# A 3x3 convolution moved into the next image's attention stretch, and the scan's sums, gather and output projection queued one step later

## The chip, the core and the metric

The kernel runs on one core of a Trainium2 chip. Its engines have a queue of instructions each, worked off in order: PE (matrix products, into PSUM), DVE (vector work), ACT (activations, with a table that must be loaded for some functions), POOL (vector work and indirect DMAs), SP (here only DMA issues). The metric is device microseconds for one execution, the median of several runs.

## What is computed

An image has 256 channels of 32 x 32 points, and there are four. Layer one is, for every image:

```python
xn = layernorm(xs)                                   # over channels
xm = mamba_v(xc, ...) + skip_scale * xc              # 4 groups of 64 channels, scan over 1024 points
Q  = conv1d(conv1d(x_concat, qdw), qpw); xg = sigmoid(Q) * xm
R  = conv1d(conv1d(xgt, rdw), rpw) + xgt
xm2 = conv1d(conv1d(cat, fdw), fpw) + cat[:, :Cc]
x_local  = conv1d(xm2, lc)
x_global = mha(xm2)                                  # 8 heads of 32
x_out = gelu(layernorm(concat(x_local, x_global) @ fc_w.T))
xi = conv3x3_depthwise(ln_hw(x_out))
x  = x + layernorm(xi) @ proj_w.T
```

Layer two is a mixture of eight experts with two chosen for each of the 4096 points: a gate picks them, and each expert is 256 to 1024, gelu, 1024 to 256. The scan is h = dA * h + dBu over the points, 128 inner channels times 16 states for each group.

## The kernel before

**Scan.** An image is 8 parts: 4 groups (n), 2 halves (h) of 512 points. A part is 16 steps (`scan`, L631): a step multiplies dt*u by B on DVE (L538), runs the scan instruction on DVE (L545) and multiplies by C on POOL (L550, and L549 keeps the last column in the first half). dA comes from ACT (L531). Every fourth step, `sums_of` (L552) adds up states on PE (L556). Around this, tables written by hand say at which step of a part other pieces are queued: `before` (L583) holds the finish of the part before (last sums, `gather` L561 with a POOL multiply, `project_out` L568, `add_skip` L573), `behind` and `group` what the next part needs.

**Everything else** is written as Python generators: each `yield n` ends a piece, and the next piece is issued n beats later. `beat()` (L1166) moves all running generators on; a scan step is followed by one beat. So the order on each engine's queue is fixed when the program is built. Buffers come from pools with tags: "a8" (8 buffers of 128 x 2048), "a4" (7), "a2" (17 of 128 x 512: dA, hs, the exponentials e of attention, squares), and 8 PSUM banks.

**Order of an image b.** In the first four parts of image b the scan runs beside `convolutions(b-1)` (L684): the depthwise passes of L360 and the rdw, rpw, fdw, fpw products. At the end of part 3 the scan stops, and `attention(b-1)` (L842) runs in 32 steps: logits on PE (L861), exponentials on ACT (L871), values on PE (L903), pair sums on DVE (L913), column sums on PE (L881). Beside it run `local(b-1)` (L927), the end of part 3, and `normalised(b+1)` (L382). When step 29 is queued the flag "attended" is set and the scan goes on with parts 4 to 7. `mixing(b-1)` (L936) follows attention in the same generator: output projection and fc (L947 to L967), a layer norm and gelu (L990 to L998), statistics (L1001 to L1014), the 3x3 taps (16 DVE instructions, L1035), a second layer norm, the projection and the residual (L1049 to L1071), and the dispatch of the image's rows to experts (L1414): transposes, gate, places, and 16 indirect DMAs on POOL (L1539).

**Tail.** `tiles` (L1081) starts in the last part of image 3. It loads expert weights, reads 256 rows (L1688), transposes them (L1734) and runs a tile: 32 products (L1757), gelu on ACT (L1762), 32 products (L1767), and two indirect adds on POOL (L1778). 35 tiles run this way, in series of 8, 8 and 23 less 4: the first series needs images 0 and 1 counted and sent, the second image 2, the third image 3. `known` and `sent` (L1088, L1091) test that, and a tile that isn't loaded polls every fourth beat. After the scan, `convolutions(3)` runs beside the tiles; then the flag "hold" stops the tiles, `attention(3)` runs, and `mixing(3)` runs beside the tiles again, with the speed of the tiles against it set by `PACE`. Tile 15 is held until image 3 is sent.

Of the kernel before, what the change touches and what calls it, by code (L numbers as in the profile page):

```python
# [10 lines left out]
AF = mybir.ActivationFunctionType  # L11
ALU = mybir.AluOpType
# [4 lines left out]
NC2 = C // P  # L17
# [54 lines left out]
def network(  # L72
# [27 lines left out]
    nc = tc.nc  # L100
    shifted = sums is None
    B = x.shape[0]
# [25 lines left out]
    eps5 = cpool.tile([P, 1], F32, name="eps5")  # L128
# [14 lines left out]
    with tc.tile_pool(name="w_conv", bufs=1) as wp, tc.tile_pool(  # L143
        name="act8", bufs=8
    ) as act8, tc.tile_pool(name="act4", bufs=7) as act4, tc.tile_pool(
        name="act2", bufs=17
    ) as act2, tc.tile_pool(name="steps", bufs=2) as actd, tc.tile_pool(
        name="steps4", bufs=6
    ) as acts, tc.tile_pool(name="rows", bufs=3) as actc, tc.tile_pool(
        name="small", bufs=1  # L150
    ) as small, tc.tile_pool(
        name="spread", bufs=2, space=bass.MemoryType.DRAM
# [23 lines left out]
        for i in range(4):  # L176
            at = _AT["qk_b"] + i // 2
# [58 lines left out]
        GD, GS = DIN // 32, DS // 4  # L236
# [62 lines left out]
        def a8(name):  # L299
            return act8.tile([P, NC2, N], F32, tag="a8", name=name)  # L300
# [127 lines left out]
        T = {}  # L428
# [144 lines left out]
        def add_skip(b, n, h):  # L573
# [7 lines left out]


        before = {  # L583
            1: [(sums_of, GS - 1)], 3: [(gather,)], 6: [(project_out,)], 8: [(add_skip,)],
        }

        behind = {
# [43 lines left out]
        def scan(at, i, stop):  # L631

            b, n, h = parts[at]
            q, g = divmod(i, GD)
            if at > 0:
                for what, *args in before.get(i, ()):
                    if parts[at - 1] not in finished:
                        what(*parts[at - 1], *args)
            if at + 1 < len(parts):
                for what, *args in behind.get(i, ()):  # L640
                    if what is not spread_b or not stop:
                        what(*parts[at + 1], *args)
            nb, nn = (b, n + 1) if n + 1 < NB else (b + 1, 0)
            if nb < B:
                for what, *args in group[h].get(i, ()):
                    what(nb, nn, *args)
            if g == 1 and q + 1 < GS:
                spread_b(b, n, h, q + 1)
            if g == 0 and q + 1 < GS:
                spread_c(b, n, h, q + 1)  # L650
            if g == 1 and q > 0:
                sums_of(b, n, h, q - 1)
            ahead = i + LEAD
            if ahead < NSTEP:
# [272 lines left out]
        def local(b):  # L927

            yield 3
            XLOC[b] = a8(f"xloc_{b}")  # L930
            for c in range(NC2):
                yield from depthwise3(XLOC[b], c, XM2[b], c, "lc_w", c, col("lc_b", c))
            del XM2[b]


        def mixing(b):  # L936

            xloc, oT = XLOC.pop(b), OT.pop(b)
            xglo = a8(f"xglo_{b}")

            def pace(ticks):

                if b == B - 1:
                    T["pace",] = ticks

            pace(PACE["product"])
            yield from in_turn(  # L947
                CO_H, lambda at: product(
                    f"ao_{b}_{at[0]}_{at[1]}", aoutT_s, at[0],
# [4 lines left out]
                ),  # L954
            )

            xc = a8(f"xc_{b}")
            both = (xloc, xglo)
            yield from in_turn(
                CO_H, lambda at: product(  # L960
# [5 lines left out]
                ),  # L966
            )  # L967

            def inverse_deviation(name):
                r = a4(f"r_{name}")  # L970

                def squares(h):
                    sq = [a2(f"sq_{name}_{h}_{c}") for c in range(NC2)]
                    for c in range(NC2):
                        nc.scalar.activation(sq[c], xc[:, c, half(h)], AF.Square)
                    return sq

                for h in range(2):
                    sq = squares(h)
                    yield 1  # L980
                    var = column_mean(f"var_{name}_{h}", sq)
                    yield 2
                    root(r[:, half(h)], var, eps5)
                    yield 1
                yield 1
                for c in range(NC2):
                    nc.vector.tensor_tensor(xc[:, c, :], xc[:, c, :], r, ALU.mult)
                    yield 1

            pace(PACE["norm"])  # L990
            yield from inverse_deviation(f"lgn_{b}")
            for c in range(NC2):
                nc.scalar.activation(
                    xc[:, c, :], xc[:, c, :], AF.Gelu, bias=col("lgn_b", c), scale=col("lgn_w", c)
# [2 lines left out]
            log_exp()  # L997
            yield 2  # L998


            mv = small.tile([P, NC2, 2], F32, tag="mv", name=f"mv_{b}")  # L1001
            for c in range(NC2):
                st = small.tile([P, 2, 6], F32, tag="bn", name=f"bn_{b}_{c}", bufs=2)
# [8 lines left out]
                rs[:, :, 1:2], mv[:, :, 0:1], -1.0, rs[:, :, 0:1], ALU.mult, ALU.mult  # L1012
            )
            yield 1  # L1014
            xi = a8(f"xi_{b}")
            xz = []
            pace(PACE["taps"])
            for c in range(NC2):
                xz.append(
                    act4.tile([P, HH, WW], F32, tag="a4", name=f"xz_{b}_{c}")  # L1020
# [17 lines left out]
                    )  # L1038
                    yield 1 if k % 2 else 0

            xc = xi

            def centre(h, mean):
                for c in range(NC2):
# [1 line left out]
                        xc[:, c, half(h)], xc[:, c, half(h)], mean, ALU.subtract  # L1046
                    )

            pace(PACE["norm"])  # L1049
            xr = a8(f"xr_{b}")  # L1050
            nc.sync.dma_start(xr, x[b].rearrange("(c p) n -> p c n", p=P))
            yield from in_turn(
# [4 lines left out]
            yield from inverse_deviation(f"fin_{b}")  # L1057

            def residual(at, r):
                co, h = at  # L1060
# [11 lines left out]
            pace(PACE["rows"])  # L1072
# [5 lines left out]
            pace(1)  # L1078


        def tiles():  # L1081
# [81 lines left out]
        def start(*what):  # L1163
            running.extend([tick, w] for w in what)
# [17 lines left out]
        def one_by_one(*what):  # L1182
            for w in what:
                yield from w

        def flagged(what, *flag):
            yield from what
            T[flag] = True
# [10 lines left out]
        PACE = {"product": 3, "norm": 1.7, "taps": 0.67, "rows": 1.6}  # L1199
        with tc.manual_schedule(engines=ALL):  # L1200
            log_exp()
            start(normalised(0), weights())
            drain()
            first_part()
            for b in range(B):
                for p in range(PARTS):
                    at = b * PARTS + p
                    stop = b > 0 and p == PARTS // 2 - 1 or at == len(parts) - 1
                    if b == 0 and p == 2:
                        start(normalised(1))  # L1210
                    if b > 0 and p == 0:
                        start(convolutions(b - 1))
                    if at == len(parts) - 1:
                        start(tiles())
                    for i in range(NSTEP):
                        scan(at, i, stop)
                        if b > 0 and p == 0 and i == 9:
                            whole(b - 1)
                        beat()
                    if b > 0 and p == PARTS // 2 - 1:  # L1220
                        drain()
                        behind_ = [attention(b - 1), mixing(b - 1)]
                        start(one_by_one(*behind_), finish_part(at), local(b - 1))
                        if b + 1 < B:
                            start(normalised(b + 1))
                        while not T.get(("attended", b - 1)):
                            beat()
                        resume(at + 1)
            T["scanned",] = True
            start(  # L1230
                flagged(finish_part(len(parts) - 1), "whole", B - 1),
                flagged(convolutions(B - 1), "convolved"),
            )
            until("convolved")
            T["hold",] = True
            until("held")
            start(flagged(attention(B - 1), "attended", B - 1, 2), local(B - 1))
            until("attended", B - 1, 2)
            T["hold",] = False
            start(mixing(B - 1))  # L1240
            drain()

    if not shifted:
# [23 lines left out]
class Experts:  # L1267
# [10 lines left out]
    T = 256  # L1278
# [627 lines left out]
```

## Time and profile before

| | us |
|---|---|
| median of 3 runs (2509.42 to 2511.86) | 2511.09 |
| the profiled execution | 2513.66 |
| its span, first to last instruction | 2511.8 |
| PE, DVE, ACT, POOL busy | 2124.0, 1632.1, 1192.2, 1160.5 |
| scan from its first step to its last | 81.2 to 1723.3 |
| parts with an attention in them (images 1, 2, 3) | 129.8, 129.8, 117.9 |
| tail | 1723.3 to 2511.8 |

How to read the lines that follow. A line of the stretch view has the stretch (us from the span's start), its length, and then for each engine the busy us and the instructions; behind that the granted PE clock, the share of the DMA engines and GB/s. A line of the group view has the line of the kernel, engine, operation, output and inputs by name, shapes and count; behind the bar the busy us and the mean ns of one; behind the second bar the idle time just ahead of them. PE's busy time is modelled for pipelined products, so that a full PE need not be at its peak.

### The profile page before, as it was taken

To read this page: it belongs to the slowest core of one execution; us is meant where nothing else is said; L and a number is where in the kernel's file an instruction comes from. 1 tells how busy PE (TensorE), PEld (TensorE's weight loads), DVE (VectorE), ACT (ScalarE), POOL (GpSimd) and SP (SyncE) were. 2 spreads that over 40 slices of the span, in tenths; PEclk is the share of its full clock that TensorE was granted. 3 is DMA by queue.
4 is the path that set the end of the run, shared out by engine and by line. 5 is a ranking of instruction groups with operands and counts; after the bars stand their busy time and mean duration, and the time that the engine had idled before them with its cause. 6 is when DMAs were issued, how large, how long until landed. Compare 5 with 4: busy or idle time off the path is not lost. (4 is left out here: it accounts for less than half of the span.)

```text
span 2511.8 us, 28315 instructions
## 1 busy us (share of the span) xinstructions
PE 2124.0 (85%) x8810; PEld 945.7 (38%) x8810; DVE 1632.1 (65%) x2243; ACT 1192.2 (47%) x2014; POOL 1160.5 (46%) x1163
## 2 busy tenths in 40 slices
PE   5776778899977879997786999758899999699995
PEld 2111111333312213331221322214674366588884
DVE  2688898875799997578999766897324434311111
ACT  1544455368645534776444478632325853222221
POOL 2577777541576595146758613663421011322221
PEclk8788897899978879998787999979999999899997
DMA  3443342320233233022342210333443034666664
GB/s 94 98 112 96 85 117 70 73 68 26 51 89 98 72 102 89 9 59 65 85 110 85 66 42 22 81 108 123 142 112 89 1 93 143 192 194 193 193 197 147
DMA packets 154540, 244.17 MB, mean 97 GB/s; under 512 B 34016, under 2 KB 103300, under 8 KB 154376
## 3 DMA queue, kind: packets, MB, share of 16 engines
q1 hardware_dynamic: 133856, 215.46, 30.4%
q0 software_dynamic: 13744, 19.31, 3.8%
q10 hardware_dynamic: 6776, 7.45, 0.9%
q8 instruction: 74, 1.21, 0.2%
q14 instruction: 90, 0.74, 0.1%
HBM read 141.16 MB, written 33.85 MB: 70 GB/s over the span
## 5 line engine op out<-in xcount | busy, mean ns | idle before, releaser
L550 POOL TENSOR_TENSOR hs<-hs,cs 128x512 f32<-128x512 f32 x512 | 687.6, 1344 | 215.7 <-DVE hs L545 160.0
L531 ACT ACTIVATE dA<-dts,A 128x512 f32<-128x512 f32 x512 | 344.5, 715 | 285.2 <-DMA dts<-dt 191.0
L556 PE MATMUL yp<-hs,quads 128*32 128x512 f32 x1024 | 317.4, 677 | 162.2 <-POOL hs L550 124.0
L538 DVE TENSOR_TENSOR dBu<-dts,bs 128x512 f32<-128x512 f32 x512 | 348.6, 681 | 67.3 <-DMA dts<-dt 24.2
L1778 POOL DMA_INDIRECT Y<-ys,dest x70 | 113.5, 1622 | 582.2 <-DVE ys L1777 430.6
L545 DVE TENSOR_TENSOR_SCAN hs<-dA,last,dBu 128x512 f32<-128x512 f32 x256 | 327.7, 1280 | 24.6 <-DVE dBu L538 0.5
L545 DVE TENSOR_TENSOR_SCAN hs<-dA,dBu 128x512 f32<-128x512 f32 x256 | 312.5, 1221 | 33.5 <-ACT dA L531 8.6
L1762 ACT ACTIVATE hs<-h,b 128x256 f32<-128x256 f32 x280 | 117.2, 472 | 425.9 <-PE h L1757 222.0
L871 ACT ACTIVATE e<-st 128x512 f32<-128x512 f32 x512 | 263.4, 605 | 94.9 <-PE st L861 94.5
L1767 PE MATMUL y<-w,hs 128*128 128x256 f32 x1120 | 263.8, 388 | 8.9 <-ACT hs L1762 8.9
L1757 PE MATMUL h<-xT,w 128*128 128x256 f32 x1120 | 252.6, 381 | 0.0
L549 POOL COPY last<-hs 128x1 f32<-128x1 f32 x256 | 92.5, 361 | 311.8 <-DVE hs L545 305.1
L1767 PEld LDWEIGHTS y<-w,hs 128*128 128x128 f32 x1120 | 215.0, 195 | 46.8 <-ACT hs L1762 11.0
L913 DVE TENSOR_TENSOR e<-e,e 128x512 f32<-128x512 f32 x256 | 177.0, 753 | 79.1 <-PE av L903 61.6
L1757 PEld LDWEIGHTS h<-xT,w 128*128 128x128 f32 x1120 | 212.5, 191 | 40.6 <-issue 9.7
L1735 DVE COPY xT<-xp 128x512 f32<-128x512 f32 x35 | 24.2, 691 | 303.5 <-PE xp L1734 292.9
L523 PE MATMUL bs<-u,xpwT_s 128*32 128x512 f32 x1024 | 181.0, 677 | 35.1 <-DVE hs L545 29.9
L556 PEld LDWEIGHTS yp<-hs,quads 128*32 128x32 f32 x1024 | 52.9, 119 | 389.2 <-POOL hs L550 263.6
L861 PE MATMUL st<-qk 32*128 32x512 f32 x1024 | 188.5, 647 | 4.7 <-DVE hs L545 4.5
L439 PE MATMUL up<-xn,inwk 64*128 64x512 f32 x256 | 149.0, 733 | 18.4 <-DVE hs L545 12.3
L903 PE MATMUL av<-e,v 128*32 128x512 f32 x1024 | 141.1, 615 | 0.0
L861 PEld LDWEIGHTS st<-qk 32*128 32x128 f32 x1024 | 67.0, 185 | 125.5 <-issue 81.0
(271 smaller groups left out, 2522.9 us busy)
## 6 DMA issues: line engine op xcount, KB each, us to landing
w<-in_W_dram SPq DMA_DIRECT2D x136, 512.0 KB
dts<-dt SPq DMA_DIRECT2D x512, 128.0 KB
cs<-cd SPq DMA_DIRECT2D x512, 64.0 KB
xs<-XS SPq DMA_DIRECT2D x35, 260.0 KB
b<-in_b_dram SPq DMA_DIRECT2D x35, 128.0 KB
xn<-in_x_dram SPq DMA_DIRECT2D x4, 1024.0 KB
XL<-xl SPq DMA_DIRECT2D x8, 512.0 KB
xl<-XL SPq DMA_DIRECT2D x4, 1024.0 KB
```

The costliest lines, as they stand in the source:

```text
L439: nc.tensor.matmul(up, inwk[rows, c, k, :], XN[b][rows, c, ds(k + h * HALF, HALF)], start=(k == 0), stop=(k == KC - 1),)
L523: nc.tensor.matmul(bs[r], xpwT_s[:, n, s : s + 1].to_broadcast([P, 32]), T[b, n, "u"][:, half(h)], start=True, stop=True,)
L531: nc.scalar.activation(dA, T[b, n, h, "dts", g][:, 0, :], AF.Exp, scale=A[:, g, n, q : q + 1])
L538: nc.vector.tensor_tensor(dBu, T[b, n, h, "dts", g][:, 1, :], T[b, n, h, "bs", q], ALU.mult)
L545: nc.vector.tensor_tensor_scan(hs, T[b, n, h, "dA", i], dBu, 0.0 if h == 0 else last, ALU.mult, ALU.add)
L550: nc.gpsimd.tensor_tensor(hs, hs, T[b, n, h, "cs", q], ALU.mult)
L556: nc.tensor.matmul(T[b, n, h, "yp"][ts(g, 32)], quads, T[b, n, h, "hs", q * GD + g], start=(q == 0), stop=(q == GS - 1),)
L861: nc.tensor.matmul(sts[i], k[r, ts(kt, P)], q[r, half(h)], start=True, stop=not shifted)
L871: nc.scalar.activation(es[i], sts[i], AF.Exp, scale=1.0 / HD**0.5)
L913: nc.vector.tensor_tensor(first[i], first[i], es[i], ALU.add)
L1757: nc.tensor.matmul(hp[:, i, :], w1(c, k), xT[:, c, :], start=(c == 0), stop=(c == NC2 - 1))
L1767: nc.tensor.matmul(yp[:, ts(t, C)], hs[:, k, ts(t, P)], w2(k), start=(k == 0), stop=(k == NHC - 1))
```

## The change

`mixing` is cut in three. `joined(b)` holds the output projection, fc, layer norm and gelu; `around(b)` the statistics and the 3x3 taps; `sent_off(b)` the second layer norm, projection, residual and dispatch. `attention(b-1)` is now followed by `joined(b-1)` alone. `around(b-2)` runs behind `local(b-1)`, beside `attention(b-1)`, and for b = 2 `normalised(b+1)` is queued behind it in that generator. `sent_off(b-2)` waits for a flag: "joining" (the fc products of b-1 are queued) for image 2, "attending" (`joined` has begun) for image 3. Image 2's `around` and `sent_off` run after the scan, beside `convolutions(3)` and the first tiles; image 3's follow `joined(3)` as before. `xc` is handed on through the dictionary XC, and its buffer is held that long.

In the scan, `sums_of`, `gather`, `project_out` and `add_skip` are queued one step later, and the flag for `convolutions` with them. What each piece issues is the same.

```diff
         before = {
-            1: [(sums_of, GS - 1)], 3: [(gather,)], 6: [(project_out,)], 8: [(add_skip,)],
+            2: [(sums_of, GS - 1)], 4: [(gather,)], 7: [(project_out,)], 9: [(add_skip,)],
         }
...
-            if g == 1 and q > 0:
+            if g == 2 and q > 0:
                 sums_of(b, n, h, q - 1)
...
-        def mixing(b):
+        def joined(b):
 
             xloc, oT = XLOC.pop(b), OT.pop(b)
+            pace(b, PACE["product"])
             xglo = a8(f"xglo_{b}")
-            pace(PACE["product"])
+            T["attending", b] = True
...
-            xc = a8(f"xc_{b}")
+            xc = XC[b] = a8(f"xc_{b}")
...
+            T["joining", b] = True
+            pace(b, PACE["norm"])
+            yield from inverse_deviation(f"lgn_{b}", xc)
...
+        def around(b):
+
+            xc = XC.pop(b)
             mv = small.tile([P, NC2, 2], F32, tag="mv", name=f"mv_{b}")
...
-            xi = a8(f"xi_{b}")
+            xi = XC[b] = a8(f"xi_{b}")
...
+        def sent_off(b):
+
+            xc = XC.pop(b)
...
+        def behind_flag(flag, what):
+            while not T.get(flag):
+                yield 1
+            yield from what
...
-                        if b > 0 and p == 0 and i == 9:
+                        if b > 0 and p == 0 and i == 10:
                             whole(b - 1)
                         beat()
                     if b > 0 and p == PARTS // 2 - 1:
                         drain()
-                        behind_ = [attention(b - 1), mixing(b - 1)]
-                        start(one_by_one(*behind_), finish_part(at), local(b - 1))
-                        if b + 1 < B:
+                        start(
+                            one_by_one(attention(b - 1), joined(b - 1)), finish_part(at),
+                            one_by_one(
+                                local(b - 1), *([around(b - 2)] if b > 1 else []),
+                                *([normalised(b + 1)] if 1 < b < B - 1 else []),
+                            ),
+                        )
+                        if b > 1:
+                            flag = "attending" if b == B - 1 else "joining"
+                            start(behind_flag((flag, b - 1), sent_off(b - 2)))
+                        if b == 1:
                             start(normalised(b + 1))
...
             start(
                 flagged(finish_part(len(parts) - 1), "whole", B - 1),
                 flagged(convolutions(B - 1), "convolved"),
+                one_by_one(around(B - 2), sent_off(B - 2)),
             )
...
-            start(mixing(B - 1))
+            start(one_by_one(joined(B - 1), around(B - 1), sent_off(B - 1)))
             drain()
```

More of the change, by code (lines that the diff above doesn't have):

```diff
@@ L933, in local, with pace, inverse_deviation, squares @@
             del XM2[b]
-        def mixing(b):
+        XC = {}
+        def pace(b, ticks):
+            if b == B - 1:
+                T["pace",] = ticks
+        def inverse_deviation(name, xc):
+            r = a4(f"r_{name}")
+            def squares(h):
+                sq = [a2(f"sq_{name}_{h}_{c}") for c in range(NC2)]
+                for c in range(NC2):
+                    nc.scalar.activation(sq[c], xc[:, c, half(h)], AF.Square)
+                return sq
+            for h in range(2):
+                sq = squares(h)
+                yield 1
+                var = column_mean(f"var_{name}_{h}", sq)
+                yield 2
+                root(r[:, half(h)], var, eps5)
+                yield 1
+            yield 1
+            for c in range(NC2):
+                nc.vector.tensor_tensor(xc[:, c, :], xc[:, c, :], r, ALU.mult)
+                yield 1
+        def joined(b):
             xloc, oT = XLOC.pop(b), OT.pop(b)
+            pace(b, PACE["product"])
             xglo = a8(f"xglo_{b}")
-            def pace(ticks):
-                if b == B - 1:
-                    T["pace",] = ticks
-            pace(PACE["product"])
+            T["attending", b] = True
             yield from in_turn(
@@ L967, in mixing @@
             )
[L969 to L991, printed above, removed]
+            T["joining", b] = True
+            pace(b, PACE["norm"])
+            yield from inverse_deviation(f"lgn_{b}", xc)
             for c in range(NC2):
@@ L1014, in mixing @@
             yield 1
-            xi = a8(f"xi_{b}")
+            xi = XC[b] = a8(f"xi_{b}")
             xz = []
-            pace(PACE["taps"])
+            pace(b, PACE["taps"])
             for c in range(NC2):
@@ L1039, in mixing @@
                     yield 1 if k % 2 else 0
-            xc = xi
+        def sent_off(b):
+            xc = XC.pop(b)
             def centre(h, mean):
@@ L1047, in centre @@
                     )
-            pace(PACE["norm"])
+            pace(b, PACE["norm"])
             xr = a8(f"xr_{b}")
@@ L1056, in mixing @@
             )
-            yield from inverse_deviation(f"fin_{b}")
+            yield from inverse_deviation(f"fin_{b}", xc)
             def residual(at, r):
@@ L1071, in mixing @@
             )
-            pace(PACE["rows"])
+            pace(b, PACE["rows"])
             yield from experts.dispatch(
@@ L1077, in mixing @@
             T["sent", b] = True
-            pace(1)
+            pace(b, 1)
         def tiles():
@@ L1184, in one_by_one @@
                 yield from w
+        def behind_flag(flag, what):
+            while not T.get(flag):
+                yield 1
+            yield from what
         def flagged(what, *flag):
```

## Prediction

> **What bounds the kernel now.** I read the 40-slice table first. VectorE (DVE) is at 8 or 9 tenths until about slice 27 and PE above 9 tenths after it; only two or three slices around each attention reverse that. So there are three kinds of stretch, and a mean over the span says nothing. The chain of waits gives no help here, since it is under 1% of the span. I then took the first scan (L545) of every sixteenth step, which cuts the run into 32 parts, and asked for busy time by stretch at those borders.
>
> ```profile
> core 0: us, PE busy (x) PEld busy (x) DVE busy (x) ACT busy (x) POOL busy (x), PEclk, DMA share, GB/s
> 300.10:332.10 32.00, 25.23 (x88) 6.45 (x88) 30.30 (x35) 18.50 (x27) 26.43 (x36) 1.00 0.43 103
> 332.10:365.40 33.30, 21.23 (x73) 3.62 (x72) 31.42 (x35) 13.93 (x22) 24.11 (x20) 1.00 0.40 99
> ...
> 633.00:676.50 43.50, 42.62 (x158) 14.24 (x157) 33.36 (x38) 28.22 (x45) 26.24 (x34) 1.00 0.27 67
> 676.50:715.50 39.00, 30.07 (x96) 7.20 (x96) 36.36 (x42) 25.44 (x39) 24.99 (x19) 0.88 0.34 83
> 715.50:769.70 54.20, 43.44 (x100) 11.96 (x100) 52.59 (x56) 24.34 (x34) 41.94 (x36) 0.64 0.29 78
> 769.70:807.60 37.90, 27.63 (x99) 7.95 (x96) 36.31 (x41) 17.34 (x30) 26.51 (x20) 0.91 0.36 86
> 807.60:857.20 49.60, 43.38 (x160) 14.91 (x160) 47.51 (x79) 26.46 (x41) 30.01 (x37) 0.92 0.38 107
> 857.20:911.00 53.80, 36.82 (x96) 8.34 (x96) 52.02 (x64) 21.28 (x29) 41.69 (x46) 0.69 0.31 84
> 911.00:963.50 52.50, 43.95 (x143) 16.50 (x138) 40.39 (x43) 22.24 (x33) 36.76 (x47) 0.90 0.29 77
> 1423.90:1541.80 117.90, 116.40 (x725) 34.75 (x723) 78.39 (x103) 90.68 (x173) 26.57 (x21) 0.99 0.13 32
> ...
> 1723.30:1905.00 181.70, 175.23 (x713) 124.90 (x712) 58.41 (x164) 59.47 (x105) 49.27 (x55) 0.98 0.40 116
> ...
> 2171.00:2195.00 24.00, 4.00 (x18) 3.14 (x18) 4.59 (x19) 3.03 (x8) 15.30 (x27) 0.70 0.68 209
> ```
>
> Rows one and two are bare scan parts: 32.0 and 33.3 us, DVE busy 30.3 and 31.4. The next four are image 1's second half, where image 0's mixing runs; the three after them are image 2's first half, where the end of that pattern (the dispatch of image 1) meets the convolutions. A scan part costs what its DVE work is. Row 1423.9 is a part with attention(2) in it: DVE idles 39 of 118 us, PE does not. The last two are the tail: PE full, and one 24 us hole.
>
> ```profile
> L1035 DVE SCALAR_TENSOR_TENSOR xi<-xz,V,xi 128x961 f32<-128x961 f32 (+1 forms) x16 | 20.5, 1281 | 0.2
> L545 DVE TENSOR_TENSOR_SCAN hs<-dA,dBu 128x512 f32<-128x512 f32 x16 | 19.5, 1221 | 1.5
> L538 DVE TENSOR_TENSOR dBu<-dts,bs 128x512 f32<-128x512 f32 x16 | 11.0, 686 | 0.0
> ```
>
> This is DVE in 1624.4 to 1678.6, the part that has the 3x3 taps of image 2: 20.5 us of taps stand in line with 30.5 us of scan.
>
> **The change, part by part.** I count the generators' yields in beats; a scan step is one beat, and attention reaches "attended" after 30.
>
> *Image 1, second half.* Taps (20.5), bn_stats, final norm and residual of image 0 leave. The part with the gelu norm keeps 2 multiplies of 1.2: 33.1 + 2.4 = 35.5. The four parts go from 174.6 to 43.5 + 35.5 + 32.0 + 33.3 = 144.3: **-30.3**.
>
> *Image 2, first half.* Image 1's dispatch no longer meets the convolutions. Image 1's own first half shows them without it: 43.3 + 44.3 + 50.2 = 137.8 against 49.6 + 53.8 + 52.5 = 155.9: **-18.1**.
>
> *Taps in the attention stretch.* local takes beats 3 to 9 and around 9 to 23 of the 30. It brings DVE 16 x 1.28 + 4 bn_stats of 0.67 + 0.5 = 24 us, ACT four 1.25 us passes. In those 14 beats of about 2.7 us (86 us over 32 steps) the e sums take 28 x 0.70 = 20 us, so DVE is asked 44 us in 38: 6 over, plus a wait or two of ACT's for the statistics, behind which the next exponentials queue: +8. No row shows taps beside attention. Bounds: 0 (the 39 idle us hold it all) and 34.5 (all serial: 24 + 5.1 ACT + two waits of 2.7). The nearest row is normalised beside attention: 129.8 us with it, 117.9 without, so 12 for 5 us of DVE, 5 of ACT, 8 of PE and 13 of POOL. I keep 8 since the taps bring no PE work and need no PSUM bank.
>
> *Image 2.* normalised(3) now queues behind around(0), from beat 23, so it falls into the first scan parts. Two parts of image 0 that carry normalised(1) take 38.8 + 42.2 against 32.0 + 33.3, so 15.7; 5 hide in the idle of the part after attention (DVE 33.4 of 43.5): 10. Attention 117.9 + 8, + 10, against 129.8: **+6**. The 1 MB load and the two stores on SP move with it; nothing reads xn_3 before part 6.
>
> *Image 2, second half.* sent_off(0) starts 16 steps into the half. Centring 2.7, multiplies 2.4, residual 2.9 and the dispatch, 18.1 by the difference above, less what spills: three parts 126.3 against 131.1: **-4.8**. Its 1 MB load of x and 1 MB store to Y are SP issues as before; of 16 row scatters on POOL (1.2 us each) 9 fall into image 3's first part.
>
> *Image 3.* First half -18.1 + 3 for those nine on POOL: **-15.1**. Attention **+8**. Second half: taps out, the whole dispatch of image 1 in, 43.5 + 1 + 40.8 + 49 + 46 = 180.3 against 181.5: **-1.2**; the last part is POOL's, 29.8 + 13 scatters x 1.3.
>
> The scan ends 55.5 us earlier.
>
> *The tail.* Image 2's around and sent_off come in. PE: 16 more products of 0.47 (4 in 1.88 us) = **+7.5**; its transposes and gates were in the tail before. sent(1) is only true 61 steps into the half, so tile 0, which polls every fourth beat, begins at beat 8 of the tail instead of 1: PE waits for the last scatter (+2), its landing to the read (4.1) and read to transpose (2.7), both as at the end of the 24 us hole, and the copy: **+10**. Convolutions still end at beat 62; now 7 tiles come before the hold, not 8. The tile that is left over goes where PE has its hole, as image 3's dispatch now falls in tile 14 with 15 to cover it: **-14** of 24 (a tile is 14.2). The taps (20.5) and conv passes on DVE in the first 14 beats, and the products that wait in PE's queue for them, as the column mean does today (17.6 us in 4 waits on the taps): **+6**. Together +9.5. If the hole is not filled, it is +23.5.
>
> *Sums, gather, projection one step later.* PE waits for POOL's hs product 124 us in all, but DVE, which bounds, waits for PE only at the fpw residuals (9 to 12 us an image). I take 0; bounds -10 (3.3 us of such PE waits ahead of the last products, three images) and +5 (hs live one step more out of 17 buffers; no DVE wait on that shows now). Behind the later sums on PE stand only the next beat's products. POOL's gate multiply now shares a step with sum_dt; POOL has 6 us to spare in a bare part.
>
> **Sum**: -55.5 + 9.5 = -46. The profiled run took 2513.66 (span 2511.8 and 1.9 around it): 2467.7. The median of the runs shown, 2511.09, lies 2.6 under it: **2465**.
>
> One rule speaks against the moves. In the trace, a DVE pass of 1024 (L367) took 4.79 us while POOL ran its gate and dt products, against 1.26 free. GPSIMD Engine Reference, Specifications, of the Trainium skill says why: GpSimd's memory interfaces are shared with VectorE, and instructions with two SBUF inputs contend. The taps have two SBUF inputs, and attention leaves POOL idle, so by the rule they gain; normalised(3) goes the other way, next to the scan's POOL work. By the rule its two multiplies would double (estimate, +2.4), which the 15.7 of image 0's rows already holds.
>
> **Rivals.** *The tail gives it back.* Tail 0 filler, no hole filled, and every DVE us of image 2 (24 + 8) waited for in PE's queue: 7.5 + 10 + 24 = 41.5 instead of 9.5: 2497. For it: PE is full there and in order. Against: DVE is busy 58 of 182 us.
>
> *Taps serial with attention, slower.* The e tiles share 17 buffers; if each tap pair holds an e sum, the sum holds PE's total and that the next exponentials, every us counts: 34.5 a stretch instead of 8, and normalised(3) at its full 15.7: 2465 + 53 + 6 = 2524. It decides from 31 us a stretch (8 + 46/2). For it: DVE waits for PE's av 18 us there already, the loop is tight. Against: a sum is due a whole step later.
>
> *It doesn't do what it says.* The taps slip past "attended" into the scan: 2 x 12 more, 2489. By count they end 7 beats before.
>
> **Chances.** Forecast (2447 to 2485) 0.50; better 0.10; slipped taps 0.10; tail 0.18, a third of it within 0.2%; serial attention 0.12, of which 0.02 within. 0.2% (5 us) is about what a measurement of this kernel can tell from no change. Faster 0.50 + 0.10 + 0.10 + 0.12 = 0.82, same 0.08, slower 0.10. The range 2440 to 2510 leaves out the serial case and half of the better one.
>
> **What would show it.** Image 1's third part of its second half at 32 us, not 54; image 2's first three parts near 138; parts with attention near 126; taps inside them; first h product of tile 0 about 10 us after the last scan; 7 tiles before the last attention; the 24 us hole at 10. Wrong it is if the attention parts pass 150, or if PE in the tail shows holes that end on DVE.

## The result, and the profile after

| | before | after |
|---|---|---|
| median of 4 runs each, us | 2511.48 (2509.42 to 2516.46) | 2487.86 (2485.08 to 2492.0) |
| the profiled execution | 2513.66 | 2487.73 |
| its span | 2511.8 | 2486.0 |
| end of the scan in it | 1723.3 | 1680.7 |
| from there to the end | 788.5 | 805.3 |

The ratio of after to before is 0.9904, with an interval of [0.9884, 0.9925]: 1% faster, 23.6 us by the medians, where 46 were forecast. That is outside the forecast band (2447 to 2485) and inside the wide range (2440 to 2510). By the profiled executions the scan gave 42.6 us (forecast 55.5) and the tail took 16.8 back (forecast 9.5).

The first view to read again is busy time by stretch, at the borders that answer to those of before (the first scan of a part; the tail; the hole in it).

```profile
core 0: us, PE busy (x) PEld busy (x) DVE busy (x) ACT busy (x) POOL busy (x), PEclk, DMA share, GB/s
715.90:748.70 32.80, 29.01 (x82) 7.28 (x85) 30.29 (x35) 18.35 (x27) 26.44 (x36) 0.69 0.40 99
782.00:826.60 44.60, 35.45 (x85) 9.12 (x86) 36.30 (x39) 21.31 (x30) 31.29 (x38) 0.77 0.40 108
826.60:870.30 43.70, 33.51 (x106) 8.15 (x105) 38.98 (x40) 24.86 (x34) 31.91 (x23) 0.80 0.27 65
870.30:919.00 48.70, 44.09 (x140) 15.68 (x139) 40.44 (x44) 22.54 (x32) 29.90 (x36) 0.86 0.27 68
1173.00:1225.80 52.80, 26.89 (x80) 5.09 (x74) 50.17 (x80) 14.12 (x23) 27.76 (x29) 0.74 0.31 81
1370.20:1493.30 123.10, 122.06 (x733) 37.17 (x731) 100.19 (x127) 94.69 (x177) 26.45 (x21) 0.97 0.14 38
1680.70:1862.40 181.70, 173.46 (x651) 115.83 (x652) 82.22 (x171) 64.68 (x103) 31.50 (x25) 0.94 0.42 126
2147.20:2168.80 21.60, 0.03 (x1) 0.00 (x0) 4.55 (x19) 0.00 (x0) 3.44 (x4) 0.61 0.53 158
```

Line one is the part that had the taps, 54.2 us before and 32.8 now: its DVE work fell from 52.6 to 30.3 and its length with it. The next three are image 2's first half: 137.0 for 155.9, DVE 11 and 13 us shorter in the first two. Line 1173.0 is new: a part that is 50 of 53 us DVE, with the dispatch of image 0 in it. Line 1370.2 is attention(2) with the taps of image 1 beside it: DVE went from 78 to 100 us, the stretch from 117.9 to 123.1. The last line is a hole of 21.6 us with no product in it; before it was a stretch of 24.0 that held 4 us of products. It was to shrink to 10.

What ended that hole is read from the timeline just ahead of it:

```profile
2145.54 0.96 POOL L1561 DMA_INDIRECT XS<-XR,to  x1 [0.19 <-issue]
...
2151.17 1.56 POOL L1800 DMA_INDIRECT Y<-ys,dest  x1 [2.75 <-issue]
2152.18 0.86 POOL L1583 IOTA steps<- 128x128 f32 x1
...
2153.07 0.29 DVE L1587 TENSOR_TENSOR steps<-count,steps 128x128 f32<-128x128 f32 x1 [14.80 <-POOL steps L1583]
...
2157.86 0.14 DVE L1653 CAST used<-ends 128x1 int32<-128x1 f32 x1
2158.37 0.95 SPq L1736 DMA_DIRECT2D w<-in_W_dram  x2
...
2162.95 0.38 SPq L1710 DMA_DIRECT2D xs<-XS  x1
...
2168.87 1.11 PE L1756 MATMUL xp<-ident,xs 128*128 128x128 f32 x4 [21.64 <-DMA xs<-XS]
```

The last row scatter of image 3 (L1561) is issued at 2145.5, before PE falls idle at 2147.2. The rows are not late. What is late is the table of the third series of tiles, which says which expert and which rows a tile takes: it starts with an iota on POOL behind two adds to Y (the second at 2151.2), runs a chain of 19 small DVE instructions from 2153.1 to 2158.0, and only then can SP load weights and, at 2163.0, the rows. In the kernel before the same table was made from 2172.4 to 2178.3, while scatters went on until 2188.0, so it was not what ended the hole:

```profile
2178.15 0.14 DVE L1631 CAST used<-ends 128x1 int32<-128x1 f32 x1
...
2188.00 0.96 POOL L1539 DMA_INDIRECT XS<-XR,to  x1 [0.19 <-issue]
...
2194.80 1.11 PE L1734 MATMUL xp<-ident,xs 128*128 128x128 f32 x4 [19.36 <-DMA xs<-XS]
```

### The profile page after: what moved, and what is told of

It is laid out like the page before. It is cut to its first block, busy times and chain, and to the rows that moved or that the text cites. A ratio compares the mean times of both kernels' runs of the same rounds, so it can differ in the third digit from the quotient of the medians.

```text
span 2486.0 us, 28275 instructions
## 1 busy us (share of the span) xinstructions
PE 2132.5 (86%) x8810; PEld 940.3 (38%) x8810; DVE 1617.6 (65%) x2243; ACT 1195.0 (48%) x2016; POOL 1112.3 (45%) x1163
## 5 line engine op out<-in xcount | busy, mean ns | idle before, releaser
L550 POOL TENSOR_TENSOR hs<-hs,cs 128x512 f32<-128x512 f32 x512 | 670.5, 1312 | 225.2 <-DVE hs L545 181.7
L538 DVE TENSOR_TENSOR dBu<-dts,bs 128x512 f32<-128x512 f32 x512 | 348.2, 680 | 101.7 <-DMA dts<-dt 24.2
L556 PE MATMUL yp<-hs,quads 128*32 128x512 f32 x1024 | 298.3, 712 | 113.4 <-POOL hs L550 70.3
L1789 PE MATMUL y<-w,hs 128*128 128x256 f32 x1120 | 258.8, 382 | 4.6 <-ACT hs L1784 4.6
L523 PE MATMUL bs<-u,xpwT_s 128*32 128x512 f32 x1024 | 175.9, 710 | 49.1 <-DVE hs L545 26.9
L549 POOL COPY last<-hs 128x1 f32<-128x1 f32 x256 | 62.6, 245 | 326.2 <-DVE hs L545 308.5
L914 DVE TENSOR_TENSOR e<-e,e 128x512 f32<-128x512 f32 x256 | 170.8, 730 | 56.7 <-PE av L904 46.2
L439 PE MATMUL up<-xn,inwk 64*128 64x512 f32 x256 | 169.2, 818 | 24.9 <-DVE hs L545 18.4
L556 PEld LDWEIGHTS yp<-hs,quads 128*32 128x32 f32 x1024 | 46.7, 118 | 333.5 <-POOL hs L550 191.3
L862 PEld LDWEIGHTS st<-qk 32*128 32x128 f32 x1024 | 66.8, 185 | 123.3 <-issue 87.2
```

What stands on the lines that cost most here:

```text
L439: nc.tensor.matmul(up, inwk[rows, c, k, :], XN[b][rows, c, ds(k + h * HALF, HALF)], start=(k == 0), stop=(k == KC - 1),)
L523: nc.tensor.matmul(bs[r], xpwT_s[:, n, s : s + 1].to_broadcast([P, 32]), T[b, n, "u"][:, half(h)], start=True, stop=True,)
L538: nc.vector.tensor_tensor(dBu, T[b, n, h, "dts", g][:, 1, :], T[b, n, h, "bs", q], ALU.mult)
L550: nc.gpsimd.tensor_tensor(hs, hs, T[b, n, h, "cs", q], ALU.mult)
L556: nc.tensor.matmul(T[b, n, h, "yp"][ts(g, 32)], quads, T[b, n, h, "hs", q * GD + g], start=(q == 0), stop=(q == GS - 1),)
L862: nc.tensor.matmul(sts[i], k[r, ts(kt, P)], q[r, half(h)], start=True, stop=not shifted)
```

## Experiments

The first theory was that the moves bring in the scan what was computed, and that the difference to the forecast lies in the third series' table. The rivals were that the later sums cost it, that the taps do, or that image 2's way into the tail does. Each experiment is after or before with one edit; each ratio is to runs of before on the same chip.

**The later sums: taken back from after, and alone on before.**

```diff
-            2: [(sums_of, GS - 1)], 4: [(gather,)], 7: [(project_out,)], 9: [(add_skip,)],
+            1: [(sums_of, GS - 1)], 3: [(gather,)], 6: [(project_out,)], 8: [(add_skip,)],
...
-            if g == 2 and q > 0:
+            if g == 1 and q > 0:
...
-                        if b > 0 and p == 0 and i == 10:
+                        if b > 0 and p == 0 and i == 9:
```

> The changed kernel with the sums, the gather, the output projection and the flag for the convolutions back at their old steps. Theory: the later sums cost time, because a state product keeps its buffer one step longer and DVE then waits for PE's sums (12 us of such waits in the changed kernel, none before). Image 0, which the rest of the change does not touch, goes back from 289.7 to 284.2 us, and the whole becomes 5 to 10 us shorter: 2478 to 2483. Rival (my prediction's zero, or a gain): the 12 us of waits are paid by 21 us less waiting for the fpw products, the scan ends at 1681 or later, and the time stays at 2486 to 2495.

> The kernel before with only the sums, gather, projection and flag one step later. Theory (later sums cost): image 0 becomes 289 to 290 us long and the whole 5 to 10 us longer, 2516 to 2522. Rival (neutral or a gain): the waits for the fpw products fall from 31 us to about 10, and the time is 2500 to 2511.

Measured: 2484.52, ratio 0.9902 [0.9888, 0.9917], against after's 0.9904; and alone (the reverse edit) 2512.36, 1.001 [0.9993, 1.0026]. The later sums move the whole by nothing that can be told within some 5 us, in either company. In the parts they do act: the part with attention(0) is 127.0 with them and 129.7 without, in both kernels. In the kernel before with them alone, the three parts with an attention are 2.0 to 3.2 us shorter (127.0, 126.6 and 115.9 for 129.8, 129.8 and 117.9), and the parts around them give it back.

**The table of the third series made as soon as image 3 is counted, in after, with the sums taken back as well, and in before.**

```diff
                 s, i = order[n]
-                if i == 0:
-                    tables.append(experts.series(
-                        s, lambda name, shape: act2.tile(shape, F32, tag="a2", name=name)
-                    ))
+                table_of(s)
...
+            def table_of(s):
+                if s == len(tables):
+                    tables.append(experts.series(
+                        s, lambda name, shape: act2.tile(shape, F32, tag="a2", name=name)
+                    ))
...
             def ahead(n, at):
 
+                if len(tables) == 2 and experts.counted >= B - 1:
+                    table_of(2)
```

> The changed kernel with the tile table of the third series made as soon as image 3 is counted, and not when tile 16 is to be loaded. Theory: the hole of 21.6 us in front of tile 16 is no longer the scatters' (the last one starts at 465 us after the scan, the hole is from 466 to 488) but the table's, which stands on POOL behind the scatters and behind two indirect adds, and on SP the expert's load behind it. Then the rows of tile 16 are read about 5 us after the last scatter, the hole shrinks to 3 to 8 us and the time to 2470 to 2475. Rival: the hole is set by the scatters and the read of the rows, and stays above 15 us: 2483 to 2490.

> The changed kernel with the sums back at their old steps and the table of the third series made early. Theory: both gains add, since one lies in the scan and one in the tail: 2463 to 2470. Rival: if neither does anything, 2485 to 2490; if only the table does, 2470 to 2476.

> The kernel before with the table of the third series made as soon as image 3 is counted. Theory: here the hole in front of tile 16 (19.4 us, from 452 to 471 us after the scan) is the scatters': the last one ends at 466 and the rows are read 4 us later, while the table is done by 455; so nothing changes, 2504 to 2512. Rival: the table alone was always worth its 20 us, 2488 to 2494.

Measured: after 2465.14, 0.9824 [0.9806, 0.9841]; after with the old sums 2463.14, 0.9832 [0.9808, 0.9857]; before 2510.31, 1.0008 [0.9996, 1.002]. The edit gives after some 20 us and before nothing. (The profiled execution of the first, 2473.27, was the longest of its five; its tail is 15.0 us shorter than that of after.) In the profile of after with the early table, these are the longest gap on PE in the last tiles ahead of tile 16, and the wait for the rows of tile 16:

```profile
2135.37 4.98 PE L1794 MATMUL y<-w,hs 128*128 128x256 f32 x14 [3.43 <-ACT hs L1789]
...
2155.66 0.66 PE L1761 MATMUL xp<-ident,xs 128*128 128x128 f32 x4 [0.64 <-DMA xs<-XS]
```

3.4 us, and it ends on a gelu within tile 14; the wait for rows is 0.6 us. Tile 16 starts 478.4 us after the scan, 493.9 in after. From the first product of attention(3) to tile 16 it is 281.3 us in the kernel before, with eight tiles in between, 295.5 in after with nine, and 281.8 with nine and the early table. The theory holds: the shifted tile does fill the hole, if its table is there.

**The taps left out, in after and in before.**

```diff
                 for k in (0, 1, 2, 3, 5, 6, 7, 8):
                     ...
+                    if b >= 2:
                         nc.vector.scalar_tensor_tensor(
```

> The changed kernel without the 16 tap instructions of images 0 and 1 (the eight outer taps of the 3x3 convolution are left out for these two, their places in the order are kept), so that the attention parts of images 2 and 3 show what the taps cost there. Theory: beside attention the taps are nearly hidden, 20.5 us of DVE cost 3 to 8 us a stretch, so the parts with attention become 119 to 123 us and 116 to 120 us long, and the whole 6 to 16 us shorter than the changed kernel, 2472 to 2482. Rival (serial): each stretch becomes 15 to 20 us shorter, 2450 to 2460.

> The kernel before without the same tap instructions of images 0 and 1, so that the scan parts show what the taps cost there. Theory: DVE has no idle time in these parts, so the part with the taps falls from 54.1 to 33 to 35 us in images 1 and 2, and the whole by 38 to 43 us, to 2466 to 2473. Rival: POOL's state products or PE take their place as the bound, the parts stay above 40 us and the whole above 2480.

Both leave out the 16 outer taps of images 0 and 1. That sends other rows to other experts, and a 36th tile runs at the end where 35 did, so the whole times (2528.04 and 2513.69) compare with nothing; the parts ahead of the tail do. First the part of before that had the taps, without them, then the stretch of attention(2) of after, without them:

```profile
706.20:741.20 35.00, 31.71 (x100) 9.19 (x100) 32.89 (x40) 24.85 (x35) 26.43 (x36) 0.84 0.45 121
```

```profile
1369.90:1493.20 123.30, 122.26 (x733) 36.77 (x731) 81.19 (x110) 94.59 (x177) 26.46 (x21) 0.97 0.14 38
```

In the scan the taps cost 19.2 us of 54.2. Beside attention DVE is busy 19 us less without them (81.2 for 100.2) and the stretch is 123.3 for 123.1: they cost nothing there. The 3 to 8 us that I gave them are wrong. The 126.5 us of the part with attention(1) is the same with and without them, too.

**Image 2 back in image 3's second half, as in before.**

```diff
-                            one_by_one(attention(b - 1), joined(b - 1)), finish_part(at),
+                            one_by_one(
+                                attention(b - 1), joined(b - 1),
+                                *([around(b - 1), sent_off(b - 1)] if b == B - 1 else []),
+                            ), finish_part(at),
...
-                one_by_one(around(B - 2), sent_off(B - 2)),
```

> The changed kernel, but the statistics, taps, projection and dispatch of image 2 follow its gelu in the second half of image 3, as in the kernel before, beside the dispatch of image 1; images 0 and 1 stay one image later. Theory: in the scan they cost their DVE time (24 for around, about 8 for the norm and residual, and what of the dispatch still fits in), so image 3's second half grows from 187 to 215 to 225 us, and the tail gives back 10 to 17 us: 2500 to 2512. Rival: the tail is so full that the move of image 2 gained nothing, 2480 to 2492.

> The kernel after with the third series' table made early, and image 2's taps and dispatch back in image 3's second half. With the table late the same move gave 2489.1 beside 2487.9. Theory (image 2's place is worth little, and the table was an independent 20 us): hole on PE in front of tile 16 falls from 17 to about 4 us, whole 2468 to 2475, so image 2's place in the tail is worth 3 to 10 us beside 2465.1. Rival (the scatters set the hole again once the dispatch is in the scan, so the table gains nothing): 2485 to 2490.

Measured: 2489.14, 0.993 [0.9908, 0.9953], and with the early table 2468.08, 0.9829 [0.9801, 0.9857]. Beside after (0.9904) and after with the early table (0.9824) the move of image 2 is worth 1 to 7 us, within the intervals, no more. The scan's second half grows from 187.4 to 221.0 (+33.6), and the tail shrinks by 25.7, to 779.6. Image 2's taps stand beside image 1's dispatch there, in the longest part of the scan without attention:

```profile
1579.20:1654.50 75.30, 34.82 (x113) 12.28 (x113) 72.64 (x105) 18.63 (x29) 43.62 (x40) 0.58 0.25 69
```

The table is worth its 20 us here too (2489.14 and 2468.08): the longest gap on PE in the tiles ahead of tile 16 is 17.1 us with the late table and 3.5 with the early one.

**Image 0's scatters later.** In after, image 3's first part takes 50.4 us where image 2's takes 44.6. The waits of that part name it:

```profile
DVE dBu L538 <- DMA cs<-cd: 6.9, 1, 6.9
```

DVE stands 6.9 us for the loaded C, and in the same answer 3.8 us for POOL's dt product. Eleven scatters (13.6 us on POOL) fall into that part, six of them ahead of its dt product (L486). The edit, on after with the early table:

```diff
+        yield 11 if b == 0 else 0
```

> The kernel after with the third series' table made early (2465.1 when run alone), and image 0's 16 row scatters begun 11 beats later, so that most are queued on POOL behind the dt products of image 3's first part and not ahead of them. Theory (scatters on POOL hold up the start of that part): it falls from 50.2 us to about 45, the 6.9 us DVE wait for the loaded C and the 3.8 us wait for POOL's dt go, the next part gains 1 to 2 us; whole 2460 to 2463. Rival (POOL's work only moves, and the next part waits for the gate and dt products instead): first two parts together within 1 us of what they were, whole 2464 to 2467.

Measured: 2465.27, 0.9819 [0.9794, 0.9844], the same as with the early table alone. The rows of the two parts, with the early table alone and then with the scatters later:

```profile
1227.40:1277.60 50.20, 43.95 (x88) 10.08 (x88) 36.33 (x38) 21.41 (x30) 44.52 (x62) 0.66 0.46 128
1277.60:1321.30 43.70, 31.97 (x105) 7.78 (x104) 38.97 (x40) 24.88 (x34) 31.88 (x23) 0.84 0.28 66
```

```profile
1227.90:1272.40 44.50, 39.08 (x85) 9.67 (x86) 36.69 (x39) 21.30 (x30) 39.91 (x56) 0.65 0.47 132
1272.40:1322.80 50.40, 35.10 (x106) 8.46 (x105) 43.47 (x40) 24.87 (x34) 39.27 (x38) 0.73 0.30 78
```

The first part falls to 44.5 as the theory had it, and the second takes it all back: 93.9 and 94.9 together. The rival holds. These scatters cost some 6 us in either place.

**The statistics and taps of images 0 and 1 in the scan, all the rest moved.** For image 2 this lets `normalised(3)` back into the stretch with attention, since nothing stands ahead of it.

```diff
-                                local(b - 1), *([around(b - 2)] if b > 1 else []),
+                                local(b - 1),
...
-                            start(behind_flag((flag, b - 1), sent_off(b - 2)))
+                            start(behind_flag((flag, b - 1), one_by_one(around(b - 2), sent_off(b - 2))))
```

> The kernel after (third series' table late, as in it) with the statistics and taps of images 0 and 1 taken out of the attention stretch and put ahead of the second layer norm in the scan that follows. All the rest stays moved. Theory (a tap costs nothing beside attention and its whole DVE time in the scan): the parts with attention stay within 1.5 us of 126.5 and 123.1, the scan parts grow by 19 to 24 us an image, whole 2526 to 2536. Rival 1 (the taps hide in the waits that the moved dispatch left in the scan): 2488 to 2505. Rival 2 (taps cost 5 to 8 us beside attention, as forecast): parts with attention fall by that much, whole 2510 to 2522.

Measured: 2525.68, 1.0058 [1.0034, 1.0081], so slower than before by 0.6%. Without the new place of the taps the change is a loss. But neither theory was right in its steps. The scan ends 21.7 us later than in after, not 38 to 48; the tail is 26.6 us longer: image 1's dispatch is now so late that tile 0 starts 50.6 us after the scan and only 6 tiles come before the hold. So this run prices the place of the taps together with the dispatch that they delay. And a stretch of attention did change:

```profile
1390.50:1506.40 115.90, 115.90 (x733) 35.37 (x732) 78.36 (x103) 89.67 (x171) 26.48 (x21) 1.00 0.12 31
```

115.9 for 123.1. What `around` adds beside attention costs 7.2 us in this stretch, and the taps, as shown, none of it. (The same 115.9 stands in the kernel before with the later sums alone.)

**Where those 7.2 us are.** Cut into short pieces, the stretch of attention(2) in after shows one hole on PE, and a clock at half behind it:

```profile
1458.00:1460.00 2.00, 0.96 (x3) 0.78 (x4) 1.38 (x3) 2.00 (x4) 0.00 (x0) 0.81 0.75 182
1460.00:1466.00 6.00, 6.00 (x24) 1.12 (x25) 5.96 (x7) 2.90 (x7) 0.00 (x0) 0.50 0.28 115
```

ACT's queue ahead of it has the three passes that end a block of attention, and right behind them the pair that prepares the taps:

```profile
1456.19 1.23 ACT L1028 ACTIVATE xz<-xc,rs 128x1024 f32<-128x1024 f32 x1
...
1457.45 1.24 ACT L1033 ACTIVATE xi<-xz,V 128x1024 f32<-128x1024 f32 x1
...
1459.22 1.70 PE L862 MATMUL st<-qk 32*128 32x512 f32 x2 [1.04 <-ACT e L872]
```

From 1454.1 to 1458.6 ACT does no exponential; PE stands 1.04 us, and half clock follows from 1459.2 to 1466.0. Counted so, some 4 us of the 7.2 are lost (1.04 and half of 6.8; an estimate). The experiment on after with the early table sets this pair a beat later and a beat apart, for images 0 and 1:

```diff
             for c in range(NC2):
+                if c and b < 2:
+                    yield 1
                 xz.append(
...
+                if c and b < 2:
+                    yield 1
                 nc.scalar.activation(
                     xi[:, c, :], ...
```

> The kernel after with the third series' table made early (2465.1 when run alone), and in the two attention stretches the second pair of ACT passes that prepare the taps (xz and xi of 1.23 and 1.24 us) set one beat later and one beat apart, so that it no longer follows the three passes that end a block of attention. Theory (what the moved piece costs beside attention is this pair: exponentials come 4.6 us late, PE stands 1.04 us and is then granted 0.7 of its clock for some 10 us): the hole on PE and the low clock go, the parts with attention fall from 126.5 and 123.3 us to 120 to 123 and 117 to 120, whole 2455 to 2461. Rival 1 (the two us of ACT count wherever they are put, as ACT bounds these steps): parts within 1 us of what they were, whole 2463 to 2467. Rival 2 (two beats later the taps slip into the scan): scan parts behind attention grow by 3 us or more, whole over 2465.

Measured: 2474.31, 0.9869 [0.9842, 0.9896]. The stretches did what the theory said; this is attention(2):

```profile
1371.60:1491.20 119.60, 119.60 (x733) 37.07 (x732) 100.08 (x126) 94.53 (x177) 26.53 (x21) 1.00 0.15 39
```

119.6 for 123.3, with no hole and the clock at 1.00, and 123.5 for 126.4 in image 2. How much of the 3.7 us is the clock can be read from the run with image 2 back in image 3's second half. Its code is that of after up to the end of this stretch, and the same hole of 1.04 us stands at 1447.1, but in this execution no low clock follows:

```profile
1359.10:1481.00 121.90, 120.86 (x733) 37.23 (x732) 100.07 (x126) 94.62 (x177) 26.52 (x21) 1.00 0.14 38
```

121.9 for 123.1 in after and 123.3 with the early table: by this one execution the half clock costs 1.2 to 1.4 us, and the other 2.3 belong to the hole and to what else the pair holds up. The other 3.7 us to the 115.9 without `around` go with 5 us more of ACT work (94.5 for 89.7); no run took that apart further. The whole did not follow. In image 2 the part behind attention went from 46.4 to 54.3: it was not the taps that slipped into the scan, but more of `normalised(3)`, which queues behind them, and DVE waits 13.2 us ahead of L538 there (4.1 in after). That gives back more than image 2 won. The scan still ended 2.2 us earlier in the profiled executions (2471.62 against 2473.27), while the ratio is 0.45% above that of the early table alone. The two were measured on different chips and the profiles do not show where that would come from, so it stays open. It was not tried to shift the pair in image 3 alone.

## Where the prediction held, and where it failed

Parts are from scan start to scan start, in us, by the profiled executions (the first scan starts 0.3 earlier in after).

| step of the prediction | forecast | measured |
|---|---|---|
| image 0, image 1's first half | 0 | +6.0 |
| image 1, attention | 0 | -2.8 |
| image 1, second half | -30.3 | -28.5 |
| image 2, first half | -18.1 | -18.8 |
| image 2, attention and the part behind it | +6 | -0.4 |
| image 2, last three parts | -4.8 | +2.8 |
| image 3, first half | -15.1 | -11.7 |
| image 3, attention | +8 | +5.2 |
| image 3, second half | -1.2 | +5.9 |
| tail | +9.5 | +16.8 |

*The parts that lost work* came within 2 us of their sums: a scan part costs what its DVE work is, before and after.

*Taps beside attention.* The total was near, the working was not. In image 3 the part grew by 5.2 where 8 were forecast; the later sums take 2.0 off this part (115.9 for 117.9 by themselves), so what was moved there costs 7.2. In image 2 -0.4 stands for +6, and the later sums are 3.2 of that difference. DVE was to be asked for 6 us too many; it took all taps for nothing, at the lower bound of 0. What costs there is on ACT, for which the working had "a wait or two": 3.7 us for one pair of passes behind the end of a block, with the clock that follows, and the rest beside 5 us more of ACT work. The rival of serial attention (34.5 us a stretch) is out by a wide margin. So is that of the taps that slip into the scan, though its 2489 is near the time measured: the 32 taps of images 0 and 1 all lie in the parts with attention.

*The dispatch* is the mis-sized term of the scan. By the difference of 18.1 the three last parts of image 2 were to take 126.3; they took 133.9, and the part with the dispatch alone 52.8. DVE idles 2.6 us in that part, so its work got dearer. In the kernel before, the passes below took 3.8 us for this image. The line of image 3's part with the same work and then image 2's:

```profile
L1507 DVE TENSOR_SCALAR XR<-XR,mv,r 128x256 f32<-128x256 f32 x8 | 2.8, 398 | 0.0
```

```profile
L1507 DVE TENSOR_SCALAR XR<-XR,mv,r 128x256 f32<-128x256 f32 x8 | 7.1, 927 | 0.0
```

Eight equal passes take 7.1 or 2.8 us by where they fall against POOL's product of 1.3 us. In image 3 such waits fall on other lines (the two L1414 take 2.2 us there, 1.3 in image 2), and the eleven scatters cost some 6 us in its first half, for which 3 were forecast. I took the price from stretches where convolutions were the company, and the row of the dispatch alone did not exist. That the placement costs this is read from the trace; no run tested it by itself, except for the scatters.

*The shared interface.* The prediction weighed GPSIMD Engine Reference, Specifications, of the Trainium skill, by which the taps gain from leaving POOL's company. The runs show little of it. The 16 taps of an image took 20.5 us beside the scan and 19.8 beside attention: two of them 1.6 and 1.8 us, the others 1.2 in either place. Of the multiplies of `normalised` (L418), those of image 3, which went the other way, took 1.23 us beside the scan and 1.22 beside attention; those of image 1, also beside the scan, took 2.27 in both kernels. Where it does show is the dispatch, in small instructions that take 0.2 us elsewhere:

```profile
1207.25 1.26 POOL L550 TENSOR_TENSOR hs<-hs,cs 128x512 f32<-128x512 f32 x1 [2.67 <-DVE count L1538]
1207.27 1.32 DVE L1540 TENSOR_TENSOR acc<-acc,tot 128x64 f32<-128x64 f32 x1
```

L1540 is 0.22 us in image 3. Here it starts 0.02 us behind POOL's product and ends 0.08 us behind it. SBUF — State Buffer, section "SBUF: two separate sides", of the Trainium skill has it so: of a GpSimd instruction that reads SBUF and a VectorE instruction with two SBUF inputs, whoever starts first holds the shared ports for its whole instruction, and the other is blocked. The trace agrees for L1540. The price of such a DVE instruction next to POOL is here not a factor but the rest of POOL's instruction.

*The tail.* Up to attention(3) it was better than forecast: 2.7 us longer, where 9.3 follow from +7.5, +10, +6 and a tile of 14.2 less. Tile 0 came 14.3 us later (10), and 7 tiles ran before the hold, as counted. Of the +6 for products that wait for the taps, the profile shows 0.7 us (the column mean, L343, behind L1041). The step that failed is "-14 of 24": the leftover tile did stand where the hole was, but the hole stayed at 21.6, since the step went by what ended it before (the scatters) and not by what would be late next (the table). With the table early the step is right: the tail is 15.0 us shorter than in after, for the 14 of the step.

*Sums one step later* were taken at 0, and the whole shows 0; in the parts it is 2 to 3 us off each attention, given back around it. The step had no such terms.

*Image 0* brings 5.5 us of loss in this profile, in a part that the change's moves do not touch (38.8 to 46.1). It is no effect of the sums either: that part took 37.9 with the later sums alone and 47.6 in after with the old ones. It is chance: with the same code up to there, it took 36.4 in the run with image 2 back in the scan, at a granted clock of 0.91, and 46.1 in after at 0.67; with the old sums it was 38.8 at 0.91 and 47.6 at 0.65. So of the 12.9 us by which the scan missed its forecast in these profiles, some 6 are no part of the change. What sets the clock there was not tested.

## What to carry to other kernels

Work for an engine that bounds one stage and idles in another is worth moving whole, even into a stage that is full on PE: 20 us of taps became 0. When a hole is to be filled, list all that its end waits for, and ask which is last once the first is gone; here a table of 19 tiny instructions held 20 us. A stage that is tight on two engines does not mind a third one's work, but it minds 2.5 us at the wrong place of the second one's queue.

## What was not expected of the hardware

In a stretch in which PE was otherwise full, 1.04 us without a product was followed by a granted clock of 0.50 for 6.8 us. The same pair stands in attention(1) of after, at 999 to 1019 us (PE 8.96 of 10 us busy, then a clock of 0.68 over 10 us), and in the kernel without the taps; with the hole away the clock stayed at 1.00. In the eight kernels that have this hole in both attentions, 15 of 16 such holes were followed by a half clock, 12 of them for 6.8 us and three for 3.4. The one exception, shown above, prices the half clock at 1.2 to 1.4 us of 123.

The length of the hole alone does not decide it. In the tail of after, PE stands 2.78 us in front of a product of the last norm, and the clock behind is 1.00:

```profile
2064.50:2071.30 6.80, 6.80 (x28) 5.25 (x29) 0.00 (x0) 4.19 (x8) 0.00 (x0) 1.00 0.48 150
```

The same hole of 2.8 us was followed by a half clock in 4 of the 14 profiles, in the kernel before among them. The products on either side have 128 rows there, and the logits of attention 32; that this makes the difference is not shown. TensorE: Matmul & The Clock Gate, section "Why this matters for your kernels", of the Trainium skill warns of gaps over about 3 us. The tail mostly agrees; beside attention a third of that was enough.
